# The last tiles of two attention layers: probabilities turned by VectorE and DMA, in slots set by hand to the end

## The chip, the cores and the metric

The kernel runs on one core of a Trainium2 chip. A core has a tensor engine for matrix products (TensorE, PE in the profile; PEld is its loading of weights), VectorE (DVE), ScalarE (ACT), GpSimd (POOL) and SyncE (SP), which here only issues DMA transfers. Each engine works through its own list of instructions in order and waits on semaphores for the others. The metric is the time of one execution on the device in microseconds (us), lower is better, as the median of several runs.

## What is computed

Two layers on `x` of 8 batches x 512 tokens x 512 channels, float32, with a context `ctx` of 8 x 120 x 512. Each layer is a gated cross-attention from the tokens to the context and a gated feed-forward part. The first layer routes tokens to experts, the second is a channel mix with a mask in its attention:

```python
x = x + tanh(g_xattn[0]) * cross_attention(layernorm(x), ctx, ctx)            # 16 heads of 32
x = x + tanh(g_ffn[0])   * routed_experts(layernorm(x))
x = x + tanh(g_xattn[1]) * masked_cross_attention(layernorm(x), ctx, ctx, mask)  # with biases
x = x + tanh(g_ffn[1])   * channel_mix(layernorm(x))

# attention, per head
scores = q @ k.T / sqrt(32)          # 512 tokens x 120 keys
probs  = softmax(scores, axis=-1)
out    = concat_heads(probs @ v) @ Wo.T

# routed_experts, in groups of 32 tokens, 32 x 4 experts
logits = grouped @ Wc + bc
perm   = (logits == max(logits, over the 32 tokens))
result = scatter_by_perm(relu(gather_by_perm(grouped) @ W1 + b1) @ W2 + b2)

# channel_mix
out = sigmoid(xr @ W_r) * (square(relu(xk @ W_k)) @ W_v)   # xr, xk: x mixed with its previous token
```

## The kernel before

**Tiles and slots.** The 4096 tokens are 32 tiles of 128 (`NT` = 32), four of them a batch (`TB` = 4, `B` = 8 batches). `x` stays in on-chip memory. An attention layer runs through the tiles in slots, one for each tile, and a slot holds pieces of several tiles at different stages. In slot k these are: the scores of tile k (`score_products`, TensorE, L666; with a mask L656 ahead of them), their softmax, the product of the probabilities with the values for tile k-2 (`attend`, TensorE L861, then ScalarE copies its result `aT` on-chip, L869), and the output projection of tile k-3 (`output`, TensorE L878, then VectorE adds it to x, L888). The projections of the queries (L165, taken through `q7`) of the next batch are cut into pieces and put between, in slots 4 to 27; from slot 28 on there are no queries left to project. The feed-forward parts start inside the attention's slots: `after(t, stage)` calls the layer's hook `then` at named points of the slot. In layer one this is the routing of finished tiles (on TensorE L1074, on VectorE up to L1092). In layer two it is the channel mix of finished tiles (`in_slot`, with VectorE and ScalarE in `mix_chunk` L1528 and L1531).

**Turning the probabilities.** The product with the values needs the probabilities with keys along the partitions, while the softmax leaves tokens there. The kernel has two ways of turning them:

- *On TensorE* (`transpose_probs_late`): 16 transposes of 128 x 120 in four blocks (L840, into `tps`), each block in one bank of the PSUM pool `p_mm` (4 banks, shared with `aps`, `ops` and others), and a copy of each block to `prT`, on VectorE (L842) and ScalarE (L844) in turn.
- *On VectorE and by DMA* ("crossed" tiles): the softmax writes the probabilities in an order of 32 x 32 blocks. `turn_blocks` transposes all blocks of one half of the heads with one VectorE instruction (L793) and writes the half to a plane in device memory (L796, 512 KB, SyncE's queue). `fetch_blocks` reads the plane back with four DMAs (L806, 240 KB each) so that the keys lie on the partitions of `prT`. In slot k the half u = 1 of tile k is turned, and the half u = 0 of tile k-1 earlier in the same slot; tile k-1 is fetched at the end of slot k, and `attend` in slot k+1 uses it. `prT` is a tile with one buffer in both ways (`bufs=1`).

**Two forms of softmax.** `softmax` (L677, L710 maximum, L721 sixteen exponentials on ScalarE, each with its accumulated sum, L727 reciprocal on VectorE, L731 or L734 division on GpSimd) is used in the steady slots. `scores` (L738) is the form of the first slots and of the tail: one half with eight accumulating exponentials (L769), for the other half VectorE subtracts the maximum (L779), one wide exponential (L780), VectorE sums (L785).

**Which tile is turned how.** `CROSSED = range(TB, NT - TB - 2)` are the tiles 4 to 25, in both layers. `run` makes the steady slots 4 to 27 with `steady`; tiles 26 and 27 have the softmax of the steady slots, but are turned on TensorE. `tail` makes the slots 28 to 33: the first four have scores by `scores`, the last two have none and only finish tiles 29 to 31. At the start of each slot of the tail tile k-2 is turned on TensorE.

**Order.** Within the attention layers the order of instructions on each engine is the order of the program text (`tc.manual_schedule`). In `first_slots` and `run` this goes for every engine, SyncE's queue of DMA issues among them; in `tail` for the computing engines alone (`engines=compute`), and SyncE's queue there is set by a scheduler. SyncE's queue in the tails holds also the loads of the first expert weights (layer one, L1150) and of the channel mix's `wv` (layer two, L1409).

Of the kernel before, what the change touches and what calls it, by code (L numbers as in the profile page):

```python
# [18 lines left out]
B, S, D = 8, 512, 512  # L19
LK = 120  # L20
NH, HD = 16, 32
NT = B * S // P
# [8 lines left out]
MASKED = -(2.0**102)  # L31

KB, KF = 4, 30
CROSSED = range(TB, NT - TB - 2)


class Common:
# [183 lines left out]
class CrossAttention:  # L221
# [6 lines left out]

    def __init__(
        self, cm, tc, es, ins, gate, aside, mask=None, biases=None, loads=(), then=None,  # L230
        vpool=None,
    ):
# [23 lines left out]
        self.wide, self.planes = [], {}  # L256
# [420 lines left out]
    def softmax(self, t, sv):  # L677
# [4 lines left out]


        nc, soft = self.nc, self.soft
        if t - 2 in CROSSED and t in CROSSED:
            whole = self.wide.pop(0)
        else:
            whole = soft.tile([P, NC * S], FP, name="pr")
            if t in CROSSED:
                rows = whole.rearrange("p (n f) -> p n f", f=32)  # L690
                nc.gpsimd.memset(rows[:, :, KF:], 0.0)
        if t in CROSSED:
            self.wide.append(whole)
# [4 lines left out]
        crossed = t in CROSSED  # L698
        if crossed:
            half = [  # L700
                whole[:, u * 1024 : (u + 1) * 1024].rearrange(
# [36 lines left out]
    def scores(self, t):  # L738
# [3 lines left out]

        nc, soft = self.nc, self.soft
        s = self.score_products(t)
        if t in CROSSED:
            largest, exponentials, divide = self.softmax(t, s)
            for u in (1, 0):
                largest(u)
                exponentials(u)
            return [lambda: divide(1), lambda: None, lambda: divide(0)]  # L750
        pr = soft.tile([P, NC * S], FP, name="pr")[:, : NH * LK]
        pr = pr.rearrange("p (j h k) -> p j h k", h=NC, k=LK)
        sm = soft.tile([P, 4, NC], FP, name="sm")
# [93 lines left out]
    def attend(self, t):  # L847
# [3 lines left out]
        for hc in range(NC):  # L851
            for j in range(4):
                h = 4 * hc + j
                out = aps[32 * j : 32 * j + 32, hc, :]
                if t in CROSSED:
# [5 lines left out]
                nc.tensor.matmul(  # L861
                    out,
                    self.v[b // 2][:LK, b % 2, h * HD : (h + 1) * HD],
                    p,
                    start=True,
                    stop=True,
                )
# [28 lines left out]
            self.then(t, self, stage)  # L896

    def run(self):
        for k in range(TB, NT - TB):
            self.steady(k)  # L900

    def slot(self, t):
# [25 lines left out]
    def steady(self, k):  # L928

        b, f = divmod(k + TB, TB)  # L930
        crossed = k in CROSSED
        if k == TB:
            self.transpose_probs_late(k - 1)
        largest, exponentials, divide = self.softmax(k, self.score_products(k))
        for u in (1, 0):
            largest(u)
        if k - 1 in CROSSED:
            self.turn_blocks(k - 1, 0)
        done = {TB: TB - 2, TB + 1: None}.get(k, k - 3)
        if done is not None:  # L940
# [3 lines left out]
        if done is not None:  # L944
            self.after(done, "final")
        exponentials(0, range(4))
        if f == 0:
            self.begin_queries(b)
        self.q7.postponed = True
        self.q7.next()  # L950
        exponentials(0, range(4, 8))
        if crossed:
            self.turn_blocks(k, 1)
        self.q7.settle(1)
        divide(0)
        if f != TB - 1:
            self.q7.next()
        if f == 0:
# [5 lines left out]
        if k == TB:  # L964
            self.attend(k - 1)
        elif k == TB + 1:
            self.output(TB - 1, range(2))
        else:
            self.attend(k - 2)
        if k - 1 in CROSSED:  # L970
            self.fetch_blocks(k - 1)
        if k + 9 < NT:
            self.normalize(k + 9)
# [2 lines left out]

    def tail(self):

        for k in range(NT - TB, NT + 2):
            self.transpose_probs_late(k - 2)  # L980
            rest = self.scores(k) if k < NT else []
            self.output(k - 3, range(NC))
            self.after(k - 3, "final")
            self.after(k, "head")
            for part in rest:
                part()
            self.after(k, "route")
            self.attend(k - 2)
            self.after(k - 3, "late")
            self.after(k, "end")  # L990
        self.output(NT - 1, range(NC))
# [710 lines left out]
def flamingo_kernel(ctx: ExitStack, tc: tile.TileContext, a: dict, out: bass.AP):  # L1702
# [26 lines left out]
    with ExitStack() as es:  # L1729
# [5 lines left out]
        with ExitStack() as at:  # L1735
# [7 lines left out]
                attention.first_slots()  # L1743
            with tc.manual_schedule(engines=every):
                attention.run()
            with tc.manual_schedule(engines=compute):
                attention.tail()
        ffn.run()
    with ExitStack() as es:
# [3 lines left out]
        with tc.manual_schedule(engines=every):  # L1753
            attention = CrossAttention(
                cm, tc, es, [a[n] for n in ("ctx", "wq1", "wk1", "wv1", "wo1")],
                gates[:, 1:2], aside, a["mask"], (a["bqk"], a["bv"], a["bo"]), then=mix.in_slot,
            )
            attention.first_slots()
        with tc.manual_schedule(engines=every):
            attention.run()  # L1760
        with tc.manual_schedule(engines=compute):
            attention.tail()
            mix.run()


# [61 lines left out]
```

## Time and profile before

| | us |
|---|---|
| median of 3 runs | 1346.69 (1346.25, 1346.69, 1348.43) |
| profiled execution, own time | 1344.31 |
| its span | 1342.5 |
| layer one: start of the scores, slots 28 and 29 | 371.40, 380.79 |
| layer one: last output product | 423.23 |
| layer two: start of the scores, slots 28 and 29 | 980.24, 988.31 |
| layer two: last output product | 1031.85 |
| plane write (512 KB), from issue to landing, median of 88 | 3.5 |
| fetch (240 KB), from issue to landing, median of 176 | 4.1 |

The profile is of one execution, and its span is what the records cover; the time of that execution has 1.8 us around it. The granted clock of TensorE was 0.999 over the span, so durations of different places can be set beside each other. In lines of groups (part 5 of the page) the columns are: line of the code, engine, operation, what is written <- what is read, partitions x elements and type, count | busy time and mean of one, idle time of the engine just ahead of them and what ended most of it. In lines of the timeline they are: start in us from the span's start, duration, engine, line, operation; in brackets at the end, where there is one, the time that the engine stood idle ahead of it and the instruction that ended the wait.

### The profile page before, as it was taken

The numbers are of one execution on the slowest core, as the hardware profiler recorded it, in microseconds if no ns is written. First come the engines' busy times: TensorE is split into PE (matmuls) and PEld (weight loads), VectorE is DVE, ScalarE is ACT, GpSimd is POOL, SyncE is SP. The second block draws the span as 40 slices with busy tenths as digits, with TensorE's granted clock in tenths as the row PEclk, the third lists the DMA queues.
The fourth block names the chain that finished last, engine by engine and source line by source line (L and its number), as shares of the span: only waits on it lengthen the run. The fifth ranks groups of instructions, "written<-read, shape, count | busy, mean of one in ns | idle before, by whom it ended". The sixth has DMA issues, their size and how long they took to land. (4 is left out here: it accounts for less than half of the span.)

```text
span 1342.5 us, 32823 instructions
## 1 busy us (share of the span) xinstructions
PE 1291.0 (96%) x13184; PEld 1024.3 (76%) x13184; DVE 1002.2 (75%) x1448; ACT 807.1 (60%) x2540; POOL 704.6 (52%) x626
## 2 busy tenths in 40 slices
PE   7999999999999988999999999999999999999997
PEld 6886777777766877888888667667666888888886
DVE  5876776777685776777887687777785778787776
ACT  1368888888774445455136778888774655544442
POOL 4856655565542002555797787777664333343332
PEclk9999999999999999999999999999999999999999
DMA  9501766766603256431410077767700000000000
GB/s 313 189 1 66 224 208 204 222 211 208 198 26 111 86 171 199 128 112 63 154 47 18 33 229 214 220 212 222 223 23 1 16 17 32 32 32 32 32 32 32
DMA packets 116237, 160.84 MB, mean 120 GB/s; under 512 B 6973, under 2 KB 71997, under 8 KB 116085
## 3 DMA queue, kind: packets, MB, share of 16 engines
q1 hardware_dynamic: 116085, 158.75, 37.1%
q8 instruction: 104, 1.70, 0.5%
q14 instruction: 48, 0.39, 0.1%
HBM read 93.84 MB, written 64.88 MB: 118 GB/s over the span
## 5 line engine op out<-in xcount | busy, mean ns | idle before, releaser
L721 ACT ACTIVATE pr<-s,nmx 128x120 f32<-128x120 f32 x768 | 273.5, 498 | 43.4 <-DVE nmx L710 25.1
L878 PE MATMUL ops<-wo,aT 128*128 128x512 f32 x512 | 237.0, 604 | 3.6 <-ACT aT L869 2.3
L731 POOL TENSOR_TENSOR pr<-pr,rs 128x960 f32<-128x960 f32 x88 | 160.1, 1820 | 139.9 <-DVE rs L727 138.0
L721 ACT ACTIVATION_READ_ACCUMULATOR pr<-s,nmx 128x1 f32 x768 | 195.3, 254 | 0.0
L878 PEld LDWEIGHTS ops<-wo,aT 128*128 128x128 f32 x512 | 91.9, 189 | 99.8 <-issue 89.2
L710 DVE TENSOR_REDUCE nmx<-s 128x8 f32<-128x960 f32 x96 | 106.6, 1153 | 57.9 <-PE s L666 57.8
L1353 POOL TENSOR_TENSOR r<-r,b 128x1024 f32<-128x1024 f32 x31 | 73.5, 2377 | 145.1 <-ACT r L1352 145.1
L793 DVE STREAM_TRANSPOSE pr<-pr 128x1024 f32<-128x1024 f32 x88 | 109.1, 1240 | 37.0 <-POOL pr L731 37.0
L165 PE MATMUL qps<-xnT,wq 128*128 128x256 f32 x512 | 119.0, 380 | 0.0
L165 PEld LDWEIGHTS qps<-xnT,wq 128*128 128x128 f32 x512 | 96.3, 189 | 23.3 <-issue 10.3
L52 DVE BATCH_NORM_STATS2 bnst<-x 128x6 f32<-128x512 f32 x128 | 87.5, 684 | 0.4
L1609 POOL TENSOR_TENSOR x<-x,cv 128x512 f32<-128x512 f32 x30 | 44.0, 1466 | 79.0 <-DVE cv L1606 79.0
L759 POOL TENSOR_TENSOR pr<-pr,rs 128x960 f32<-128x960 f32 x32 | 58.1, 1823 | 40.6 <-DVE rs L758 30.8
L861 PE MATMUL aps<-prT,v 120*32 120x128 f32 x2048 | 69.2, 276 | 7.6 <-DMA prT<-plane 3.9
L888 DVE SCALAR_TENSOR_TENSOR x<-ops,gates,x 128x512 f32<-128x512 f32 x64 | 47.8, 746 | 34.5 <-PE ops L878 34.1
L666 PE MATMUL s<-kT,qT 32*128 32x120 f32 x2048 | 71.8, 276 | 0.0
L666 PEld LDWEIGHTS s<-kT,qT 32*128 32x128 f32 x2048 | 65.7, 186 | 7.0 <-issue 4.9
L861 PEld LDWEIGHTS aps<-prT,v 120*32 120x32 f32 x2048 | 52.2, 109 | 21.2 <-issue 10.7
L1352 ACT COPY r<-rps 128x1024 f32<-128x1024 f32 x31 | 31.4, 1013 | 59.1 <-PE rps L1340 59.1
L1582 ACT ACTIVATE kT<-kT 128x512 f32<-128x512 f32 x32 | 20.0, 626 | 76.2 <-DVE kT L183 41.8
L1340 PE MATMUL rps<-ident,rT 128*128 128x128 f32 x512 | 61.9, 275 | 2.0 <-DVE rT L1320 1.7
L769 ACT ACTIVATE pr<-s,nmx 128x120 f32<-128x120 f32 x128 | 44.2, 371 | 29.0 <-DVE nmx L766 29.0
(239 smaller groups left out, 3134.4 us busy)
## 6 DMA issues: line engine op xcount, KB each, us to landing
plane<-pr SPq DMA_DIRECT2D x88, 512.0 KB, 3.5
prT<-plane SPq DMA_DIRECT2D x176, 240.0 KB, 4.1
w<-in_w_dram SPq DMA_DIRECT2D x32, 512.0 KB, 5.0
x<-in_x_dram SPq DMA_DIRECT2D x8, 1024.0 KB, 16.6
aside<-x SPq DMA_DIRECT2D x32, 256.0 KB, 3.1
x<-aside SPq DMA_DIRECT2D x8, 1024.0 KB, 9.7
out_dram<-x SPq DMA_DIRECT2D x14, 512.0 KB, 2.8
wk<-in_wk_dram SPq DMA_DIRECT2D x3, 1024.0 KB, 8.8
```

Source lines behind the costliest of these rows:

```text
L52: cm.nc.vector.bn_stats(st, cm.x[:, t, :])
L165: self.nc.tensor.matmul(ps[:, m, :], rows[:, k, m * n : (m + 1) * n], columns[:, k, :], start=(k == 0), stop=(k == 1),)
L666: nc.tensor.matmul(s[j // 2][:, j % 2, hc * LK : (hc + 1) * LK], self.qT[b][r : r + 32, hc, toks], self.kT[r : r + 32, hc, keys], start=no ...
L710: nc.vector.tensor_reduce(nmx[u], sv[u], AX.X, ALU.max, negate=True)
L721: nc.scalar.activation(dst, src, AF.Exp, bias=nmx[u][:, j, hc, :], accum_out=sm[:, u, j, hc : hc + 1],)
L731: nc.gpsimd.tensor_tensor(half[u], half[u], by, ALU.mult)
L759: nc.gpsimd.tensor_tensor(pr[:, js, :, :], pr[:, js, :, :], rs[:, js, :, :].to_broadcast([P, 2, NC, LK]), ALU.mult,)
L793: nc.vector.transpose(pr, pr)
L861: nc.tensor.matmul(out, self.v[b // 2][:LK, b % 2, h * HD : (h + 1) * HD], p, start=True, stop=True,)
L878: nc.tensor.matmul(ops, self.aT[t][:, c, :], self.wo[:, c, :], start=(c == 0), stop=(c == NC - 1),)
L1340: nc.tensor.transpose(ps[:, k // 4, (k % 4) * P : (k % 4 + 1) * P], self.rT[:, 16 * tq + 8 * h + k, :], self.cm.ident,)
L1353: nc.gpsimd.tensor_tensor(r, r, b2, ALU.add)
```

## The change

Tiles 26 to 31 of layer one and tiles 29 to 31 of layer two are crossed too, as tiles 4 to 25 are; in layer two tiles 26, 27 and 28 are still turned on TensorE. The set of crossed tiles becomes an argument of each layer's attention. `run` goes on to the last tile, so that slots 28 to 31 are steady slots: scores, then the steady softmax with its sixteen exponentials, and the output product ahead of the exponentials' later parts; the parts that project queries are left out there (`b < B`). `tail` keeps the two slots without scores (32 and 33), which now turn the second half of tile 31 and fetch tile 31 in slot 32. It stands under `every`, so that SyncE's queue follows the program there too. The buffers of probabilities are handed on from tile t-2 to tile t by number instead of by a list, since the crossed tiles of layer two have a gap; `memset` clears the padding of a block where a buffer is newly taken.

```diff
-CROSSED = range(TB, NT - TB - 2)
+CROSSED = range(TB, NT)
...
     def softmax(self, t, sv):
...
-        if t - 2 in CROSSED and t in CROSSED:
-            whole = self.wide.pop(0)
-        else:
+        crossed = t in self.crossed
+        whole = self.wide.pop(t - 2, None) if crossed else None
+        if whole is None:
             whole = soft.tile([P, NC * S], FP, name="pr")
-            if t in CROSSED:
+            if crossed:
                 rows = whole.rearrange("p (n f) -> p n f", f=32)
                 nc.gpsimd.memset(rows[:, :, KF:], 0.0)
...
     def scores(self, t):
...
         s = self.score_products(t)
-        if t in CROSSED:
-            largest, exponentials, divide = self.softmax(t, s)
-            for u in (1, 0):
-                largest(u)
-                exponentials(u)
-            return [lambda: divide(1), lambda: None, lambda: divide(0)]
...
     def run(self):
-        for k in range(TB, NT - TB):
+        for k in range(TB, NT):
             self.steady(k)
...
     def steady(self, k):
...
-        crossed = k in CROSSED
-        if k == TB:
-            self.transpose_probs_late(k - 1)
+        crossed = k in self.crossed
+        turned = k - 1 if k == TB else k - 2
+        if k != TB + 1 and turned not in self.crossed:
+            self.transpose_probs_late(turned)
         largest, exponentials, divide = self.softmax(k, self.score_products(k))
         for u in (1, 0):
             largest(u)
-        if k - 1 in CROSSED:
+        if k - 1 in self.crossed:
             self.turn_blocks(k - 1, 0)
...
-        if f == 0:
+        if f == 0 and b < B:
             self.begin_queries(b)
-        self.q7.postponed = True
-        self.q7.next()
+        if b < B:
+            self.q7.postponed = True
+            self.q7.next()
         exponentials(0, range(4, 8))
...
     def tail(self):
-        for k in range(NT - TB, NT + 2):
-            self.transpose_probs_late(k - 2)
-            rest = self.scores(k) if k < NT else []
+        for k in (NT, NT + 1):
+            if k - 2 not in self.crossed:
+                self.transpose_probs_late(k - 2)
+            if k - 1 in self.probs and k - 1 in self.crossed:
+                self.turn_blocks(k - 1, 0)
             self.output(k - 3, range(NC))
             self.after(k - 3, "final")
             self.after(k, "head")
-            for part in rest:
-                part()
             self.after(k, "route")
             self.attend(k - 2)
+            if k - 1 in self.planes:
+                self.fetch_blocks(k - 1)
             self.after(k - 3, "late")
...
             with tc.manual_schedule(engines=every):
                 attention.run()
-            with tc.manual_schedule(engines=compute):
                 attention.tail()
...
                 gates[:, 1:2], aside, a["mask"], (a["bqk"], a["bv"], a["bo"]), then=mix.in_slot,
+                crossed=(*range(TB, NT - TB - 2), *range(NT - 3, NT)),
             )
             attention.first_slots()
         with tc.manual_schedule(engines=every):
             attention.run()
+            attention.tail()
         with tc.manual_schedule(engines=compute):
-            attention.tail()
             mix.run()
```

More of the change, by code (lines that the diff above doesn't have):

```diff
@@ L230, in __init__ @@
         self, cm, tc, es, ins, gate, aside, mask=None, biases=None, loads=(), then=None,
-        vpool=None,
+        vpool=None, crossed=CROSSED,
     ):
@@ L255, in __init__ @@
         self.xn, self.xnT, self.qT, self.probs, self.aT = {}, {}, {}, {}, {}
-        self.wide, self.planes = [], {}
+        self.crossed, self.wide, self.planes = crossed, {}, {}
         self.ops = {}
@@ L684, in softmax @@
         nc, soft = self.nc, self.soft
-        if t - 2 in CROSSED and t in CROSSED:
-            whole = self.wide.pop(0)
-        else:
+        crossed = t in self.crossed
+        whole = self.wide.pop(t - 2, None) if crossed else None
+        if whole is None:
             whole = soft.tile([P, NC * S], FP, name="pr")
-            if t in CROSSED:
+            if crossed:
                 rows = whole.rearrange("p (n f) -> p n f", f=32)
                 nc.gpsimd.memset(rows[:, :, KF:], 0.0)
-        if t in CROSSED:
-            self.wide.append(whole)
+        if crossed:
+            self.wide[t] = whole
         sm = soft.tile([P, 2, 2, NC], FP, name="sm")
@@ L697, in softmax @@
         self.probs[t] = whole
-        crossed = t in CROSSED
         if crossed:
@@ L744, in scores @@
         s = self.score_products(t)
-        if t in CROSSED:
-            largest, exponentials, divide = self.softmax(t, s)
-            for u in (1, 0):
-                largest(u)
-                exponentials(u)
-            return [lambda: divide(1), lambda: None, lambda: divide(0)]
         pr = soft.tile([P, NC * S], FP, name="pr")[:, : NH * LK]
@@ L854, in attend @@
                 out = aps[32 * j : 32 * j + 32, hc, :]
-                if t in CROSSED:
+                if t in self.crossed:
                     at = (NC * j + hc) * 32
@@ L955, in steady @@
         divide(0)
-        if f != TB - 1:
+        if f != TB - 1 and b < B:
             self.q7.next()
-        if f == 0:
+        if f == 0 and b < B:
             self.sum_tokens(2)
@@ L963, in steady @@
             self.transpose_x(k + 8)
-        if k == TB:
-            self.attend(k - 1)
-        elif k == TB + 1:
+        if k == TB + 1:
             self.output(TB - 1, range(2))
         else:
-            self.attend(k - 2)
-        if k - 1 in CROSSED:
+            self.attend(turned)
+        if k - 1 in self.crossed:
             self.fetch_blocks(k - 1)
```

## The prediction

> **What bounds the kernel now.** Read first are the span and the engines' shares, then the chain that ended last around the ends of the two attention layers, then TensorE in order of time there.
>
> ```profile
> span 1342.5 us, 32823 instructions
> PE 1291.0 (96%) x13184; PEld 1024.3 (76%) x13184; DVE 1002.2 (75%) x1448; ACT 807.1 (60%) x2540; POOL 704.6 (52%) x626
> ...
> 1023.92 3.44 PE ops L878 x8
> 1027.35 1.73 PE cps L165 x8
> 1029.08 1.01 PE aps L861 x32
> ```
>
> TensorE is busy 96% of the span, and the chain (start, length, instructions) runs on it through the end of layer two. What the change touches lies in two stretches: 361 to 427 us (layer one) and 980 to 1036 us (layer two). Next, TensorE in time, a tail slot of layer one and then the last matmuls of both layers:
>
> ```profile
> 388.29 1.96 PE L840 MATMUL tps<-ident,pr 128*120 128x128 f32 x16
> 390.18 1.17 PE L666 MATMUL s<-kT,qT 32*128 32x120 f32 x32
> 391.28 3.70 PE L878 MATMUL ops<-wo,aT 128*128 128x512 f32 x8
> ...
> 423.23 3.70 PE L878 MATMUL ops<-wo,aT 128*128 128x512 f32 x8 [0.70 <-ACT aT L869]
> ...
> 1031.85 3.60 PE L878 MATMUL ops<-wo,aT 128*128 128x512 f32 x8
> ```
>
> Slots are back to back: scores start at 371.40, 380.79, 390.18, 399.57, so 9.39 us each, 1.89 of it the transposes (388.29 to 390.18). The slots of layer two start at 980.24, 988.31, 996.45, 1004.60. I follow the time from there to the last output product, which starts at 423.23 and 1031.85: gather and channel mix hang on it, so a shift of it carries to the end.
>
> **What goes.** Tiles 26 to 31 of layer one and 29 to 31 of layer two lose 16 transposes each: 9 x 1.89 = 17.0 us of TensorE. Were nothing else in the way, 1344.31 (the profiled execution) would become 1327.3. With them go copies (0.69 us twice on VectorE, 0.59 twice on ScalarE a tile). The tail's softmax goes too: 8 accumulating exponentials, one wide one (0.90) and VectorE's subtraction and sum (1.16, 1.15). Tiles 28 to 31 of both layers get 16 exponentials, issued every 0.336 us (321.75, 322.10, 322.44 in slot 23): 5.4 us for about 3.6.
>
> **What comes, and its loops.** A turned tile brings two VectorE transposes (1.24 us), two plane writes (0.36 us of SP each) and four fetches (0.87 us of SP each, 3.48 together). Slot 23 is such a slot already, without a gap on TensorE:
>
> ```profile
> 320.56 2.22 DVE L710 TENSOR_REDUCE nmx<-s 128x8 f32<-128x960 f32 x2 [1.38 <-PE s L666]
> 325.10 1.82 POOL L731 TENSOR_TENSOR pr<-pr,rs 128x960 f32<-128x960 f32 x1 [4.65 <-DVE rs L727]
> 326.95 1.25 DVE L793 STREAM_TRANSPOSE pr<-pr 128x1024 f32<-128x1024 f32 x1 [0.31 <-POOL pr L731]
> 328.22 0.36 SPq L796 DMA_DIRECT2D plane<-pr  x1
> 328.82 4.51 SPq L806 DMA_DIRECT2D prT<-plane  x4
> 328.87 0.29 DVE L1092 TENSOR_TENSOR permT<-rlps,lmx 128x128 f32<-128x128 f32 x1
> ```
>
> VectorE waits in order for GpSimd's division before its transpose; behind it stand the second reciprocal, the routing operations (to 329.16) and the next maximum. From 320.56 that is a loop of 8.65 us, which a slot cannot beat, though TensorE would need only 7.0 to 7.5. SP is the second loop: the fetch of the previous tile is queued behind the plane write, 8.2 us after the maximum, and SP's next plane waits behind the fetch. How long a fetch takes:
>
> ```profile
> 894.05 3.48 SPq L806 DMA_DIRECT2D prT<-plane  x4
> 901.35 1.08 PE L861 MATMUL aps<-prT,v 120*32 120x128 f32 x32 [0.36 <-DMA prT<-plane]
> ...
> DMA to landing us min/median/max: 3.6/3.7/3.7
> ```
>
> From the first issue to the product that waited: 7.3 us. The last line is the fetch at 360.84, with no plane written beside it: the last issue comes 2.66 us after the first, plus 3.7, 6.4 us. The worst is 5.1 (at 972.3, beside a 1 MB load), 7.8 us. I take 7.3 where a plane is in flight, 6.4 for the last tile, and both ends for the range. Two slots then take 8.2 + 7.3 + 1.0 (attend) + 1.3 (scores to maximum) = 17.8, or 8.9 a slot.
>
> The page "DMA: Bandwidth & Descriptors" of the Trainium skill, section "Anatomy of one DMA", fits 2.0 us plus bytes/436e3 (written for GpSimd's path). For 240 KB that is an estimate of 2.6 us, against 3.6 to 5.1 here; by it the whole sum would end at about -2.5 us, and I stay with the rows.
>
> **Layer one.** Scores 28 start 1.89 us earlier, 369.5, their maximum 1.25 later, 370.75. At 8.9 a slot the maximum of tile 31 is at 397.5, against 400.81: 3.3 gained. Now the short slots. prT has one buffer, so a fetch cannot start before the product that reads the tile before. Fetch 29 starts at 388.6 + 8.2 = 396.8, its product runs 404.1 to 405.1; fetch 30 at 397.5 + 8.2 = 405.7, product 413.0 to 414.0; fetch 31 at 414.1, product 420.5 to 421.5. Between these TensorE has only the output (3.54) and routing (1.42), and idles. After the copy of aT (0.7) the last output starts at 422.2, not 423.23: **-1.0 us**. With 6.4 everywhere (slots then 8.65) it is -2.6, with 7.8 +1.4.
>
> **Layer two.** Slots 28 and 29 still transpose tiles 27 and 28 on TensorE, and the fourth block there needs a bank that aT's copy frees:
>
> ```profile
> 993.69 1.04 ACT L780 ACTIVATE pr<-pr 128x960 f32<-128x960 f32 x1
> 994.58 0.76 ACT L1528 ACTIVATE xk<-yT,om 128x512 f32<-128x512 f32 x1
> 995.20 0.62 ACT L869 COPY aT<-aps 128x512 f32<-128x512 f32 x1
> ...
> 995.87 0.65 PE L840 MATMUL tps<-ident,pr 128*120 128x128 f32 x4 [0.20 <-ACT aT L869]
> ```
>
> That copy is queued behind the exponentials, now 1.8 us longer, and the scores behind the transposes. Slot 28: maximum at 981.59 as before, exponentials 982.8 to 988.2, chunk and copy to 989.4, block, scores 29 at 990.0 (+1.7). Slot 29 likewise: maximum 991.3, exponentials 992.5 to 997.9, scores 30 at 999.75 (+3.3). Slot 30 has nothing to transpose after it: scores 31 at 1007.8 (+3.2). Then the waits of layer one: fetch 29 at 1009.4, product 1016.7 to 1017.7; output and two channel-mix pieces (0.65 + 3.54 + 3.45) to 1025.4, which covers fetch 30; product to 1026.4; fetch 31 6.4 later, product 1032.9 to 1033.9, one piece (1.8), last output 1035.7 against 1031.85: **+3.85 us**. With 6.4 it is +2.95, with 7.8 +5.8.
>
> **At nothing:** two more memsets in layer two (0.21 us each, GpSimd idles 1.40 before such divisions; uncovered 0.4 us); the load of wv, now behind fetch 25 on SP (used 40 us later, at 1016.78; it may lift the 0.73 wait at 977.33, but a copy to 979.4 holds the scores anyway); the first w1 load, now behind fetch 31 (used at 445.71; uncovered it would hold the first expert products back by the shift itself).
>
> The page "VectorE: DVE Perf Modes", section "Rules for kernel authors", gives full 128x128 transposes to TensorE, since VectorE turns only 32x32 blocks. The rows agree where the round trip shows (6.4 to 7.8 us against 1.89) and not where other products cover it; by the rule alone every one of the nine tiles would lose.
>
> **Sum:** -1.0 + 3.85 = +2.85. On the profiled execution 1344.31 gives 1347.2; the runs' median, 1346.69, lies 2.4 above that execution, so 1349.5 as a median. From the ends: +0.35 to +7.2.
>
> **Rivals.** *Fetches stay covered, faster.* For it: 88 turned tiles waited only four times, 3.9 us in all. Against: their slots had 1.7 to 3.5 us of query pieces for cover. Price: layer one at 8.65 a slot and short slots of TensorE's own work, last output at 416.4 (-6.8); layer two keeps +3.2 at scores 31, loses two transposes (3.8) and gains three waits for aT (0.65): +1.35. Together -5.5: 1341.2.
> *Fetches slow down, slower.* In both tails, planes, fetches and writes of x share the queues in shorter slots; if the last landing is 5.1 us and not 4.6, each loop grows: 1.4 + 5.8 = +7.2, 1353.9. It decides from about 4.9. For it: the 972.3 case; against: that one had 1 MB beside it.
> *Layer two's loss is taken up later, no change.* TensorE waits 1.37 us for ScalarE at 1043.73. If that absorbs it: 2.85 - 1.4, 1348.1. Against: ScalarE's work there hangs on the same last products.
>
> **How the numbers follow.** No change means within 0.2%, 2.7 us (1344.0 to 1349.4), about what these runs can tell. Forecast 0.53, half of it on each side of 1349.4 (same 0.25, slower 0.28); covered 0.18, faster; slow fetches 0.17, slower; taken up 0.12 (same 0.10, faster 0.02). Faster 0.20, same 0.35, slower 0.45. The range, 1342.0 to 1354.0, leaves out half of the covered case and a little above the slow one; the forecast's own is 1347.0 to 1351.5.
>
> **What would show it.** Right: in layer one slots of 8.7 to 9.1 us with no L840, TensorE waiting for prT (L861) 1 to 4 us ahead of each of the last two products; in layer two scores 30 and 31 about 3 us later, the last transpose block waiting for aT. Wrong: TensorE without gaps in the short slots, slots below 8.6, or scores 29 of layer two at 988 as before.

## The result, and the profile after

| | before | after |
|---|---|---|
| median (lowest to highest) of 16 runs each, us | 1346.75 (1344.89 to 1354.67) | 1352.80 (1348.07 to 1363.75) |
| profiled execution, us | 1344.31 | 1356.36 |
| its span, us; granted clock | 1342.5; 0.999 | 1354.3; 0.988 |
| layer one: output product of slot 27 to last output product | 61.42 | 64.14 |
| between the two ends | 546.31 | 545.74 |
| layer two: scores of slot 27 to last output product | 62.31 | 71.84 |
| from there to the end | 310.65 | 310.94 |

The ratio of the times is 1.0046 [1.0027, 1.0064]: slower, by 6.05 us in the medians, where 2.85 were forecast. The four stretches are read from the starts of TensorE's products; they show that the loss sits in the two places that the change touches, most of it in layer two. What the prediction has no word for stands in the page of the kernel after:

```profile
span 1354.3 us, 32755 instructions
PE 1287.3 (95%) x13040; PEld 1016.8 (75%) x13040; DVE 994.3 (73%) x1432; ACT 812.0 (60%) x2642; POOL 706.1 (52%) x628
...
PEclk9999999999998999999999999999989999999999
```

The removed transposes are gone from TensorE's busy time only in part (1291.0 to 1287.3, not 17 less), and the row of the granted clock has an 8 in two slices, 406 to 440 and 982 to 1016 us: there TensorE ran below its clock, and its remaining products took longer. TensorE in order of time at layer one's end (start, duration, line; in brackets the wait and its releaser):

```profile
386.59 1.08 PE L854 MATMUL aps<-prT,v 120*32 120x128 f32 x32 [2.21 <-DMA prT<-plane]
387.60 2.08 PE L666 MATMUL s<-kT,qT 32*128 32x120 f32 x32
389.61 4.39 PE L871 MATMUL ops<-wo,aT 128*128 128x512 f32 x8
...
405.51 1.08 PE L854 MATMUL aps<-prT,v 120*32 120x128 f32 x32 [2.80 <-DMA prT<-plane]
...
414.30 1.39 PE L854 MATMUL aps<-prT,v 120*32 120x128 f32 x32 [1.98 <-DMA prT<-plane]
416.38 6.35 PE L871 MATMUL ops<-wo,aT 128*128 128x512 f32 x8 [0.69 <-ACT aT L862]
...
423.99 1.08 PE L854 MATMUL aps<-prT,v 120*32 120x128 f32 x32
425.78 3.70 PE L871 MATMUL ops<-wo,aT 128*128 128x512 f32 x8 [0.70 <-ACT aT L862]
```

The transposes (L833 now) are gone, and the waits for `prT` have come as forecast. New is what follows some of the waits: the same scores take 2.08 instead of 1.17 us, the same output 6.35 instead of 3.70. Busy time by windows of 3.41 us (window, its length, busy time of each engine with its instructions; then the granted clock, the DMA share and GB/s):

```profile
384.20:387.61 3.41, 1.20 (x36) 0.85 (x35) 2.25 (x6) 2.62 (x12) 3.02 (x5) 1.00 0.85 290
387.61:391.03 3.42, 3.42 (x38) 2.62 (x35) 1.33 (x3) 1.49 (x3) 1.07 (x1) 0.50 0.86 264
411.51:414.92 3.41, 1.43 (x32) 1.22 (x34) 1.98 (x6) 0.59 (x1) 1.06 (x3) 1.00 0.90 305
414.92:418.33 3.41, 2.72 (x22) 1.24 (x12) 0.00 (x0) 1.40 (x2) 0.00 (x0) 0.50 0.31 93
418.33:421.75 3.42, 3.42 (x6) 1.35 (x5) 0.00 (x0) 0.00 (x0) 0.00 (x0) 0.50 0.73 219
```

In a window in which TensorE was busy 1.20 or 1.43 of 3.41 us the clock is still 1.00, and in the next it is 0.50. The edges of all stretches at half clock lie on one grid of 3.413 us. In the execution before there was no such stretch up to 1338.93, when TensorE's last product (to 1335.1) is over. In the one after there were 27.3 us of them: 10.2 in layer one's end, 13.7 in layer two's, 3.4 in the expert stage. Over the 16 runs of the kernel after, time and granted clock go together (correlation -0.93): from 1348.07 at 0.997 to 1363.75 at 0.985, 1.3 us for each 0.001. The wider spread of its runs goes with that.

In layer two TensorE waits for other things (same columns):

```profile
991.45 0.84 PE L833 MATMUL tps<-ident,pr 128*120 128x128 f32 x4 [2.04 <-ACT aT L862]
...
994.43 5.76 PE L871 MATMUL ops<-wo,aT 128*128 128x512 f32 x8
...
1012.99 0.58 PE L656 MATMUL s<-mbias,ones 1*128 1x480 bf16 x2 [2.36 <-ACT pr L720]
...
1015.20 5.61 PE L871 MATMUL ops<-wo,aT 128*128 128x512 f32 x8
```

The fourth transpose block waits for the copy of `aT`, as forecast, and the scores of tile 31 wait for the exponentials; each of the two waits is again followed by an output at half clock. But VectorE in order of time shows that the first of these slots would be long without that too. First the kernel after, then the same place in the kernel before:

```profile
990.96 2.01 DVE L1526 SCALAR_TENSOR_TENSOR xk<-yT,mu,xk 128x512 f32<-128x512 f32 x1 [0.41 <-ACT xk L1523]
992.89 1.27 DVE L835 COPY prT<-tps 120x512 f32<-120x512 f32 x2
994.58 2.22 DVE L709 TENSOR_REDUCE nmx<-s 128x8 f32<-128x960 f32 x2 [0.42 <-PE s L666]
1000.23 0.75 DVE L881 SCALAR_TENSOR_TENSOR x<-ops,gates,x 128x512 f32<-128x512 f32 x1 [3.43 <-PE ops L871]
...
1003.02 1.25 DVE L786 STREAM_TRANSPOSE pr<-pr 128x1024 f32<-128x1024 f32 x1 [1.93 <-POOL pr L730]
...
1006.09 2.21 DVE L709 TENSOR_REDUCE nmx<-s 128x8 f32<-128x960 f32 x2
```

```profile
987.92 0.70 DVE L1531 SCALAR_TENSOR_TENSOR xk<-yT,mu,xk 128x512 f32<-128x512 f32 x1
988.54 1.28 DVE L842 COPY prT<-tps 120x512 f32<-120x512 f32 x2
989.74 1.15 DVE L766 TENSOR_REDUCE nmx<-s 128x8 f32<-128x960 f32 x1
```

The maxima of slot 28 start at 983.48, those of slot 29 at 994.58 and of slot 30 at 1006.09: 11.1 and 11.5 us, where the kernel before took 8.15. Between the first two stand, in series, the sixteen exponentials (984.72 to 990.1), ScalarE's part of the channel mix (0.81), VectorE's part (2.01; it took 0.70 before, and here a division of GpSimd runs from 990.63 to 992.42) and the copies of the turned blocks (1.27). VectorE is free for the next maximum only at 994.16; the scores at half clock hold it 0.42 longer. Between the second two half clock has a larger part: VectorE, in its order, waits 3.43 us for the output at half clock, and the reciprocal, GpSimd's division, the block transpose of tile 29, the mix (0.70 here) and the copies stand behind that.

### The profile page after: what moved, and what is told of

Its sections match the earlier page's. It is cut to its first block, busy times and chain, and to the rows that moved or that the text cites. A ratio compares the mean times of both kernels' runs of the same rounds, so it can differ in the third digit from the quotient of the medians.

```text
span 1354.3 us, 32755 instructions
## 1 busy us (share of the span) xinstructions
PE 1287.3 (95%) x13040; PEld 1016.8 (75%) x13040; DVE 994.3 (73%) x1432; ACT 812.0 (60%) x2642; POOL 706.1 (52%) x628
## 5 line engine op out<-in xcount | busy, mean ns | idle before, releaser
L730 POOL TENSOR_TENSOR pr<-pr,rs 128x960 f32<-128x960 f32 x106 | 193.7, 1827 | 180.8 <-DVE rs L726 178.2
L871 PE MATMUL ops<-wo,aT 128*128 128x512 f32 x512 | 244.7, 620 | 6.4 <-ACT aT L862 5.1
L720 ACT ACTIVATION_READ_ACCUMULATOR pr<-s,nmx 128x1 f32 x896 | 228.3, 255 | 0.0
L871 PEld LDWEIGHTS ops<-wo,aT 128*128 128x128 f32 x512 | 94.8, 195 | 108.6 <-issue 94.0
L709 DVE TENSOR_REDUCE nmx<-s 128x8 f32<-128x960 f32 x112 | 124.3, 1152 | 61.6 <-PE s L666 61.6
L786 DVE STREAM_TRANSPOSE pr<-pr 128x1024 f32<-128x1024 f32 x106 | 131.4, 1240 | 50.8 <-POOL pr L730 50.8
L666 PE MATMUL s<-kT,qT 32*128 32x120 f32 x2048 | 75.0, 283 | 0.0
L666 PEld LDWEIGHTS s<-kT,qT 32*128 32x128 f32 x2048 | 68.5, 193 | 7.2 <-issue 4.8
L1345 DVE TENSOR_TENSOR r<-rps,b 128x1024 f32<-128x1024 f32 x33 | 40.4, 1225 | 28.2 <-PE rps L1335 28.1
L1335 PEld LDWEIGHTS rps<-ident,rT 128*128 128x128 f32 x512 | 55.5, 141 | 7.5 <-issue 4.8
```

Source lines behind the costliest of these rows:

```text
L666: nc.tensor.matmul(s[j // 2][:, j % 2, hc * LK : (hc + 1) * LK], self.qT[b][r : r + 32, hc, toks], self.kT[r : r + 32, hc, keys], start=no ...
L709: nc.vector.tensor_reduce(nmx[u], sv[u], AX.X, ALU.max, negate=True)
L720: nc.scalar.activation(dst, src, AF.Exp, bias=nmx[u][:, j, hc, :], accum_out=sm[:, u, j, hc : hc + 1],)
L730: nc.gpsimd.tensor_tensor(half[u], half[u], by, ALU.mult)
L786: nc.vector.transpose(pr, pr)
L871: nc.tensor.matmul(ops, self.aT[t][:, c, :], self.wo[:, c, :], start=(c == 0), stop=(c == NC - 1),)
```

## The experiments

Two theories stood from here. *Clock*: the waits cost about what was forecast, and the rest is TensorE at half clock after windows that the waits left poor. *Waits alone*: half clock is a symptom that costs nothing of its own. The stretches below are those of the table above. A kernel with only one layer changed keeps the other as it was; each ratio is to runs of the kernel before on the same chip. Where the tail's program is that of before, layer one's end took 61.41 or 61.42 us in five profiles and layer two's 62.24 to 63.43 in five, so one microsecond in layer two's end says little.

| kernel | layer one's end | at half clock | layer two's end | at half clock | ratio to before |
|---|---|---|---|---|---|
| before | 61.42 | 0 | 62.31 | 0 | |
| after | 64.14 | 10.2 | 71.84 | 13.7 | 1.0046 [1.0027, 1.0064] |
| layer_one_alone | 61.65 | 6.8 | 63.43 | 0 | 1.0003 [0.9989, 1.0018] |
| layer_two_alone | 61.42 | 0 | 69.25 | 6.8 | 1.0075 [1.0054, 1.0096] |
| fill | 61.21 | 0 | 71.92 | 6.8 | 1.0033 [1.0022, 1.0045] |
| one_to_27 | 61.16 | 0 | 62.53 | 0 | 0.9982 [0.9971, 0.9992] |
| holes_short | 65.14 | 0 | 62.64 | 0 | 1.0022 [1.0011, 1.0032] |
| holes_long | 72.46 | 13.7 | 62.24 | 0 | 1.0051 [1.0032, 1.0070] |
| early_copy | 61.41 | 0 | 71.37 | 6.8 | 1.0057 [1.0039, 1.0074] |
| max_first | 61.42 | 0 | 67.15 | 3.4 | 1.0062 [1.0041, 1.0083] |
| two_all_turned | 61.41 | 0 | 72.15 | 13.7 | 1.0056 [1.0035, 1.0076] |
| one_early_fetch | 65.76 | 9.5 | 63.26 | 0 | 1.0063 [1.0041, 1.0085] |
| both_27_early | 62.22 | 0 | 69.56 | 10.2 | 1.0083 [1.0057, 1.0109] |
| both_to_27 | 61.53 | 0 | 66.11 | 6.8 | 1.0011 [0.9999, 1.0023] |

### The two halves of the change

A slot number `end` was added, at which `run` stops and `tail` with `scores` begins:

```diff
-        for k in range(TB, NT):
+        for k in range(TB, self.last):
             self.steady(k)
...
 # layer_one_alone, layer two's attention (layer_two_alone: the same for layer one)
+                crossed=range(TB, NT - TB - 2), end=NT - TB,
```

> Only layer one is changed; layer two ends as before. Theory A (clock): the waits of layer one cost what the forecast's low end says, so its last output product would start 2.4 us early at full clock (-2.4), but a window in which TensorE idles some 2 us is followed by one or two stretches of 3.4 us at half clock, about 2.5 us each on average in the profile after: median 1348, granted clock spread over 0.992 to 0.998, and each run 1.3 us longer for each 0.001 of clock lost. Rival (the forecast as it stands, waits alone): 1345.7, all runs at the clock of before, 0.9987. Rival C (the loss sits in layer two alone): 1344.3, clock 0.9987.

> Only layer two is changed; layer one ends as before. Theory A (clock): +3.7 us from the late copy of aT and the fetches, and on top some 3 us on average from stretches at half clock after slots 28/29 and 31: median 1353, clock 0.991 to 0.997. Rival (waits alone): +3.85 us, 1350.6, clock 0.9987 in all runs. Rival C: the whole difference, 1352.8.

Layer one alone changes nothing that can be told: 1348.54 against 1348.50. Its end took 61.65 us with one stretch of 6.8 us at half clock:

```profile
406.31 1.94 PE L855 MATMUL aps<-prT,v 120*32 120x128 f32 x32 [2.32 <-DMA prT<-plane]
408.94 5.66 PE L872 MATMUL ops<-wo,aT 128*128 128x512 f32 x8 [0.69 <-ACT aT L863]
...
415.86 1.08 PE L855 MATMUL aps<-prT,v 120*32 120x128 f32 x32
```

The value product took 1.94 instead of 1.08 and the output 5.66 instead of 3.70, 2.8 us more. Not all of that lengthens the end, since the fetch that the product at 415.86 reads landed at 414.93: of the output's 1.96 only 0.93 can be saved. By these rows half clock cost an estimated 1.8 us, and without it the end would be about 1.6 us shorter than before. What the layer gains is given back by the clock (0.9930 as a mean over its runs, 0.9963 for the kernel before on that chip). By the time alone the rival without the clock (0.9992) is not excluded either; the trace decides. Layer two alone costs 1358.63 against 1348.50, 10.1 us, where the three expectations allowed 6.3 at most (1353 against 1346.75). The two ratios multiply to 1.0078, above the 1.0046 of both together; they are from other executions, and each mean hangs on the clock that its runs met.

### Does half clock cost time of its own?

In the kernel before, ScalarE writes the bank of a value product of layer one some times ahead of it, so that TensorE waits:

```diff
         aps = self.p_mm.tile([P, NC, P], FP, name="aps", tag="mm")
+        for _ in range(0 if self.masked else {26: 4, 28: 4}.get(t, 0)):
+            self.nc.scalar.copy(aps.rearrange("p c f -> p (c f)"), self.wo[:, 0, :])
 # holes_short: {26: 1, 27: 1, 28: 1, 29: 1}
```

> The kernel before, with TensorE made to wait in four slots of layer one's tail (one copy by ScalarE into the bank of the value product ahead of it, some 1.5 us each, 6.0 in all). Theory A (a window of 3.4 us with under half of it busy brings half clock): holes this short leave enough, so +6.0 and no more: 1354.5, granted clock as before. Rival (any wait brings it, or none): the same lost time beyond the holes as in holes_long.

> The kernel before, with the same waiting time of TensorE in two holes instead of four (four copies each, some 3.2 us each, 6.4 in all). Theory A: each hole brings one or two stretches of 3.4 us at half clock, 1.7 to 3.4 us lost on top: +9 to +13, 1358 to 1361, clock 0.003 to 0.006 lower than before. Rival (a wait costs its own length): +6.4, 1354.9, clock as before.

The four short holes were 1.22, 1.22, 1.17 and 1.17 us (4.8 in all), the two long ones 3.08 each (6.2). TensorE after a short hole, and after a long one:

```profile
380.93 1.08 PE L863 MATMUL aps<-prT,v 120*32 120x128 f32 x32 [1.22 <-ACT aps L852]
```

```profile
381.30 1.94 PE L863 MATMUL aps<-prT,v 120*32 120x128 f32 x32 [3.08 <-ACT aps L852]
383.17 3.67 PE L840 MATMUL tps<-ident,pr 128*120 128x128 f32 x16
```

After 1.22 us of waiting the value product took its 1.08 us; after 3.08 it took 1.94, and the transposes 3.67 instead of 1.96. The short holes lengthened layer one's end by 3.72, less than their sum, with no half clock in it. The long ones lengthened it by 11.04, 4.9 more than theirs, with two stretches of 6.83 us. The holes came out shorter than expected. In the profiles the rival, that a wait costs its own length, falls: 1.4 us more of waiting cost 7.3 us more, and the rows show where. The runs point the same way and don't decide by themselves: the medians rose by 2.5 us with the short holes and by 6.6 with the long ones (1350.24 before on that chip), so the long ones cost about their own 6.2, less than the 9 to 13 of the theory, at a mean clock of 0.9965 against 0.9932. The runs of the kernel before, at 0.9960 there, had lost clock too.

### Filling the waits

```diff
+    def fill(self, tile, n):
+        for c in range(n):
+            self.nc.tensor.matmul(
+                tile.rearrange("p c f -> p (c f)"), self.cm.ident[:, : tile.shape[0]],
+                self.wo[:, c, :], start=True, stop=True,
+            )
...
         aps = self.p_mm.tile([P, NC, P], FP, name="aps", tag="mm")
+        self.fill(aps, self.fills.get(t, 0))   # layer one {26: 1, 27: 2, 29: 2, 30: 2}, layer two {30: 1, 31: 1}
```

(with two more ahead of the third transpose block of tile 27 and three ahead of the scores of tile 31 in layer two; all are overwritten by the products that follow).

> The changed kernel, with products that nobody reads put into the waits of TensorE in both tails (each 128x512, 0.88 us at full clock; one or two at a place, where the wait was 0.9 to 3.5 us): ahead of four value products in layer one, and in layer two ahead of the third transpose block of tile 27, the scores of tile 31 and the last two value products. No wait is taken away. Theory A (clock): TensorE no longer falls to half clock there, clock 0.997 or more, median 1348.0 (the 1346.75 of before, -2.4 for layer one, +3.7 for layer two), and a narrow spread. Rival (waits alone): the added work gains nothing, 1352.8, or 1 to 3 us more where it overshoots a wait.

In layer one it did what it should for the clock: no stretch at half clock, and the mean clock of the runs 0.9955. First a place where the kernel after idled for 2.80 us, then the next value product:

```profile
403.59 1.88 PE L852 MATMUL aps<-wo,ident 128*128 128x512 f32 x4
406.38 1.08 PE L872 MATMUL aps<-prT,v 120*32 120x128 f32 x32 [0.91 <-DMA prT<-plane]
...
414.83 1.08 PE L872 MATMUL aps<-prT,v 120*32 120x128 f32 x32
```

The end of layer one took 61.21 us against 64.14, but not the 59 of the theory. The filling itself is not the reason: at three of its four places the fetch came 0.35 to 0.91 us after it, and for the product at 414.83 it landed at 414.69; the last product, without filling, waited 1.46 us. At full clock too the fetches set the pace, and what is left of the gain is 0.2 us. In layer two it failed: the wait at the transposes moved from tile 27, where the filling stood, to tile 28 (2.66 us), and two stretches at half clock stayed. The time, 1353.38 against 1348.50, is 4.9 us above before, where the theory gave 1.25 (1348.0 against 1346.75). By the times alone the rival, that filling gains nothing, is not excluded (1.0033 [1.0022, 1.0045] against 1.0046 [1.0027, 1.0064]). The spread did narrow, to 3.9 us in 6 runs from 15.7 in 16. So filling restores the clock where it lies in the wait, and is no remedy.

### What sets the slots of layer two

`early_copy` moves the value product and the copy of `aT` ahead of the last four exponentials. `max_first` adds that VectorE's part of the mix of slots 27 to 29 stands behind the next tile's maxima. Both have layer two changed alone.

```diff
 # early_copy
+        else:
+            self.attend(turned)
         exponentials(0, range(4, 8))
...
-        else:
+        elif b < B:
             self.attend(turned)
...
 # max_first, in addition
         for u in (1, 0):
             largest(u)
+        while self.later:
+            self.later.pop()()   # VectorE's part of mix_chunk, put there for slots 27 to 29
```

> Layer two alone, and in its slots 28 to 31 the value product (with its copy aT) stands ahead of the last four exponentials in the order of ScalarE. Theory A (the late copy of aT holds the fourth transpose block, the hole makes the clock fall): no wait at the transposes of tiles 27 and 28 above 0.5 us; scores then wait for the exponentials instead, 8.5 us a slot; scores 29, 30, 31 at 19.0, 27.6, 36.2 us from those of slot 27 (layer_two_alone: 20.5, 31.4 and, with its second half late, 39.8), last output at 65 (69.25), no half clock in layer two's tail; median 1351 against 1358.6. Rival (the sixteen exponentials themselves or the fetches set the slots): last output at 68 to 69.5, median 1357 or more.

> early_copy, and VectorE's part of the channel mix of slots 27 to 29 put behind the maxima of the next tile. Theory A2 (in layer two a slot is one chain: maximum, sixteen exponentials, ScalarE's part of the mix, VectorE's part, the copies of the turned block, the next maximum; 10.7 to 11.1 us in the profile after, whatever TensorE does): with the mix out of it, slots of 8 to 9 us, scores 29, 30, 31 at 19, 27.5, 36.5 us from those of slot 27, last output at 64 to 65, one hole at most; median 3 to 5 us below early_copy, 1353 to 1355 at this chip's 1350 for before. Rival (fetches and half clock set the pace of layer two's tail): last output at 69 or more, no gain.

`early_copy` was a miss: the fourth block of tile 27 no longer waited, that of tile 28 waited 2.34 us with half clock behind it, and the end still took 71.37 us. VectorE in it, where no half clock has run yet:

```profile
992.91 2.01 DVE L1532 SCALAR_TENSOR_TENSOR xk<-yT,mu,xk 128x512 f32<-128x512 f32 x1 [0.41 <-ACT xk L1529]
994.85 1.27 DVE L836 COPY prT<-tps 120x512 f32<-120x512 f32 x2
996.04 2.21 DVE L710 TENSOR_REDUCE nmx<-s 128x8 f32<-128x960 f32 x2
```

The scores were there (the last two maxima start with no wait behind the copies), and the maxima still came at 984.95, 996.04 and 1007.26, 11.1 and 11.2 us apart. `max_first` breaks that chain:

```profile
992.95 1.25 DVE L836 COPY prT<-tps 120x512 f32<-120x512 f32 x2
994.15 2.22 DVE L710 TENSOR_REDUCE nmx<-s 128x8 f32<-128x960 f32 x2
996.28 1.74 DVE L1534 SCALAR_TENSOR_TENSOR xk<-yT,mu,xk 128x512 f32<-128x512 f32 x1
```

The mix stands behind the maximum now; maxima came at 985.48, 994.15 and 1003.16, 8.7 and 9.0 us apart, and scores 29 and 30 at 18.4 and 27.1 us, as theory A2 said. So with the bank freed early, the series of exponentials, mix, copies and maximum set the slot. Moving the mix alone, with the bank as it was, was not tried. The end of the layer fell by 4.2 us, to 67.15 and not to 64: the scores of tile 31 then waited 2.79 us for the exponentials of tile 30, a value product 2.97 us for its fetch, and one stretch at half clock lay between. These waits are part of the 4.8 us that still separate it from before. The medians don't show the gain (1.0062 against 1.0057, on two chips); only the trace does.

```diff
 # two_all_turned, layer two alone
+                crossed=range(TB, NT),
```

> Layer two alone, with tiles 26, 27 and 28 turned by VectorE and DMA as well, so that no transpose and no bank wait is left in its tail. Theory A: slots of 8.7 us by the loops of ScalarE and VectorE, scores 31 at 34.8 us from those of slot 27, last output at 62.7 (before 62.3), one stretch of half clock at most: median 1349 to 1350. Rival (fetches and their queue are what costs): three more fetches, last output at 69 or more, median 1358 or more.

A miss as well. No transposes are left, and the fetches take their place on TensorE:

```profile
1004.72 1.93 PE L855 MATMUL aps<-prT,v 120*32 120x128 f32 x32 [5.17 <-DMA prT<-plane]
```

The fetch that this product waited for was issued at 996.14 behind the 1 MB load of `wv`, which held SyncE from 994.08 for 1.80 us. The rival holds: with no transposes the fetch is what is waited for.

### The order of SyncE's queue, and a smaller change

```diff
 # one_early_fetch (layer one changed alone), both_27_early
         if k - 1 in self.crossed:
             self.fetch_blocks(k - 1)
+        if crossed:
+            self.write_plane(k, 1)      # was issued in turn_blocks, ahead of the fetch
...
 # one_to_27; both_to_27 and both_27_early the same in layer two
+                    crossed=range(TB, NT - TB), end=NT - TB,
```

> layer_one_alone, and on SyncE the fetch of the tile before stands ahead of the second plane write of each slot (both layers). Theory (the fetch is queued behind that plane write, as forecast): the waits for prT of the last three value products (2.3, 0, 1.2 us) fall to 1.3, 0.8, 0.8, the last output product of layer one starts 60 us after the output of slot 27 (61.65 with one stretch of half clock), no window under half busy; 1.0 to 2.5 us below layer_one_alone. Rival (the one buffer of prT and the 6.4 to 7.3 us of the round trip set it): waits as they were, no gain.

The waits grew instead. SyncE's queue (start, time to issue):

```profile
372.93 3.47 SPq L805 DMA_DIRECT2D prT<-plane  x4
376.44 1.10 SPq L795 DMA_DIRECT2D plane<-pr  x2
382.53 3.52 SPq L805 DMA_DIRECT2D prT<-plane  x4
```

The plane that the next fetch needs is now written only when this fetch has been issued, and the next fetch starts 6.1 us later, when that plane has landed: 9.6 us from fetch to fetch, where they were 8.7 to 8.8 apart in `layer_one_alone` (372.38, 381.17, 389.92). The plane write ahead of the fetch was no queueing to be saved; it is part of the same loop. (In these two versions the order holds for the steady slots of both layers as well.)

> Layer one alone, and only tiles 26 and 27 turned by VectorE and DMA beside 4 to 25; slots 28 to 33 in the form of before (cheap softmax, tiles 28 to 31 turned on TensorE), layer two as before. Theory A: the first two transposing slots lose 1.89 us each and no wait of TensorE reaches 1.5 us, so no half clock: 1343.7 (-3.0), clock 0.9987. Rival (slots bound by VectorE's loop, 8.65 us, or SyncE's, 8.9 us, against 9.39): 2 x 0.5 to 0.7 gained, 1345.5.

> Both layers with tiles 4 to 27 turned by VectorE and DMA, the ends as before (cheap softmax, tiles 28 to 31 turned on TensorE), and the fetch ahead of the second plane write. Theory: layer one's last output at 60 us from the output of slot 27 (before 61.4, one_to_27 61.2), layer two's at 60 us from the scores of slot 27 (before 62.3: two times 1.89 less some 1.5 us of waits); no half clock in the tails: 3 to 4 us below before, ratio 0.9975. Rival (slots 28 and 29 bound by ScalarE and VectorE): layer two unchanged at 62.3, ratio 0.9985 to 1.0.

> both_27_early without its moved fetch: tiles 4 to 27 turned by VectorE and DMA in both layers, ends as before, SyncE's order as in the changed kernel. If the moved fetch was what cost there: layer one's last output 61.2 us from the output of slot 27 as in one_to_27, layer two's 62 to 63 us from the scores of slot 27 (before 62.3: VectorE, which is busy without a gap in those slots, loses 1.28 us of copies in two slots and gains two transposes), ratio 0.998. Rival (turned tiles in layer two cost wherever their fetch meets the 1 MB load of wv and its slots): layer two's at 65 or more, ratio above 1.001.

`one_to_27` is the one version that beat both kernels: 1345.93 against 1348.50, 2.6 us where the theory said 3.0 and the rival 1.2. Its layer one shows only 0.26 us of that: the two slots without transposes waited 1.54 and 1.03 us for fetches, and a later slot 1.02 for a copy. Turning tiles 26 and 27 in layer two too loses at that end: it took 66.11 us, with waits of 2.71 and 2.30 us for fetches and a stretch at half clock after each (69.56 with the moved fetch). In three executions with layer one changed and no half clock on the way, the stretch between the two ends took 543.4 to 544.2 us (`fill`, `layer_one_alone`, `both_to_27`), against 546.31 before. `both_27_early` took 547.7. What is shorter there was not settled, so where `one_to_27` gains is open.

## Why the prediction was right and where it failed

**The sign, and the range.** Slower was forecast as likeliest, and the time lies in the range of 1342.0 to 1354.0, but above the forecast's own (1347.0 to 1351.5). It came near the time of the rival *fetches slow down*, for another reason: fetches landed in 3.9 us as a median in layer one's end and 4.0 in layer two's. Only those of tile 30 in layer one came near that rival's 5.1 (5.3, 5.0, 4.7 and 4.5 us).

**Layer one, -1.0 us.** The mechanism held. The slots were 8.5 to 9.8 us apart, the maxima of tile 31 began at 398.95, some 1.6 us of it by half clock (forecast 397.5), and the products of tiles 29 and 30 waited 2.80 and 1.98 us for their fetches. That of tile 31, for which a wait was forecast too, did not wait, because the output ahead of it ran at half clock until its fetch had landed (422.37). So what half clock added to scores, value products and outputs (0.91, 0.69, 0.32, 0.31 and 2.65 us: 4.9) can't simply be taken off: of the 2.65 at most 1.6 would be saved.

The forecast's own size is best compared with executions that had less of it: 0.2 us shorter than before in `fill`, without half clock, and about 1.6 in `layer_one_alone` by the estimate above, on both sides of 1.0. The step that failed is that the idle time of the short slots was counted at its own length: it was priced as waiting, and the work after it at the durations of the full clock. The profiled end came out 2.7 us longer than before and 2.9 longer than in `fill` (64.14 against 61.42 and 61.21).

Two readings were off: one slot took 8.49 us, below the loop of 8.65 that no slot was to beat and below the 8.6 named as a sign of being wrong; and the 88 of "88 turned tiles" are plane writes, two a tile, so 44 tiles waited four times.

**Layer two, +3.85 us.** Measured +9.5 in the profiled execution and +6.9 in `layer_two_alone`. The failed step is "Slot 29 likewise: maximum 991.3". The forecast let the maximum follow the start of the scores by 1.3 us and looked at the bank behind the copy of `aT`; the maxima followed scores 29 by 2.35 us and scores 30 by 2.92. The forecast did not carry the 1.8 us of longer exponentials on to VectorE, where the mix and the copies stand ahead of the next maximum and close a loop. Scores 29 came 1.9 us later than before, as forecast (+1.7); scores 30 4.7 later (+3.3) and the second half of scores 31 6.4 later (+3.2). `early_copy` against `max_first` shows the loop. How much of layer two's loss is clock can't be told: from 991.8 on half clock ran while VectorE was busy anyway, then VectorE waited for the output that it stretched, and no execution of this end, once changed, was free of it.

**At nothing.** The extra memsets and the load of `wv` cost the changed kernel nothing that shows: behind the memsets GpSimd idled 5.59 and 1.14 us, and slot 28 of layer two began 10.53 us after slot 27, 10.70 before. The cover was thin: in `two_all_turned` the same load was waited for. The loads behind fetch 31 show no loss either: the stretch to layer two took 545.74 us, 546.31 before.

**The rivals.** *Covered* falls by the waits, *taken up later* by the last stretch, which is 0.3 us longer and not shorter. A rival was missing: that the clock falls where TensorE waits. Up to the end of TensorE's work the profile before has no window under 1.75 of 3.41 us busy and none at half clock, so it showed no price for one.

## What to carry to other kernels

A wait on an engine that is nearly always busy is not priced at its own length: look whether it leaves a window of the clock's grid less than half busy, add what the work after it takes at half clock, and take off what a later wait would have held back in any case. When work is taken from the bounding engine, follow the loop through every queue that is lengthened in exchange, here ScalarE to VectorE and back, until it closes; a loop that closes without the relieved engine is the new bound. A plane write and a fetch that alternate in one queue are one loop, and reordering them only moves the wait.

## What the runs showed of the hardware

Fourteen profiled executions were cut into windows of 3.413 us on the grid of their own clock changes. Of the windows at full clock, those followed by one at half clock (without the first microseconds and what lies behind TensorE's last products):

```
TensorE busy in the window (us of 3.41)    windows    next at half clock
under 1.3                                       17         17
1.3 to 1.5                                      12         10
1.5 to 1.7                                      13          9
1.7 to 1.9                                      20          5
1.9 to 2.2                                      68          5
over 2.2                                      5197          0
```

The granted clock was 1.00 or 0.50 and nothing between. The Trainium skill ("TensorE: Matmul & The Clock Gate", section "What's actually happening") has these two rates and a window of this length that runs free of the kernel, and the records agree. Its section "HAM oscillation — how this bites in real kernels" asks that idle gaps stay under about 3.4 us. Here gaps of 2.0 to 2.2 us were enough, where they and their neighbours fell into one window. A half-clock stretch lasted one window or two (3.41 or 6.83 us). In nine of the ten that lasted two, TensorE was busy 2.3 to 2.9 us of the first; in those of one window, 3.07 us or more, but for one at 2.70. Once it lasted two with the first fully busy (991.77 to 998.60); why was not tried. The grid lies differently in each execution: its first edge fell 0.1 to 3.3 us after the span's start. So a wait of 2 us is met in some runs and missed in others. At 130 us, far ahead of both ends, nine of the fourteen executions had a window of 1.17 to 1.65 us busy with half clock behind it, and the other five none under 1.98. That part of the program is as in the kernel before, and the times of its runs go with the clock too (on one chip from 1345.06 at 0.999 to 1353.97 at 0.995).
